# Four double PSUM pairs, keys and queries by pairs of strips, and products with ones over two chunks, in a two-layer attention kernel

## The chip, the cores and the metric

The kernel runs on one core of one Trainium2 chip. The metric is the device time of one execution in microseconds; lower is better. The engines are TensorE (PE, with its weight loads PEld), VectorE (DVE), ScalarE (ACT), GpSimd (POOL) and SyncE (SP), which here issues the DMA transfers.

## The reference

The input is 16 images of 64 x 64 positions with 256 channels, all fp32. Two pre-normalised residual layers follow each other. Cut to what matters:

```python
# layer 0: linear attention, 8 heads of 32
q, k, v = split(norm(x) @ w_qkv)
q = softmax(q, over the 32 channels of a head) * SCALE
k = softmax(k, over the 4096 positions)
context = einsum('bhdn,bhen->bhde', k, v)
x = x + einsum('bhde,bhdn->bhen', context, q) @ w_out
# layer 1: local attention in a window of 7 x 7
q, k, v = xn @ Wq + bq, xn @ Wk + bk, xn @ Wv + bv      # xn = norm(x)
score = q . (k[in window] + row or column embedding)     # emb0, emb1: half the channels each
out = x + sum over the window of softmax(score) * v      # positions outside are zero-padded
```

The norm is a group norm per image. Its mean and deviation are folded by the kernel into the weights and biases of layer 1.

## The kernel before, in words

An image is held as two tiles `img` of 128 channels x 4096 positions and handled in 8 strips of 512 positions. The order of instructions on each engine is the order of the program text; no planner moves them. A loop over the 16 images (L1018 to L1103) runs these stages one after the other:

- **Layer 0** (`layer0`). Queries and keys of two blocks of 128 positions at a time (L531), ScalarE's exponential into a `work` tile `eq` (L535), context sums (L549), the turned queries (L593 to L614), the output products (L642) and DVE's adds into `img` (L653, L656). Statistics of the strips follow, and from them mean and deviation (`group_stats`, which runs `group_steps`: products with a grouping matrix at L268 and L277, small DVE steps at L265, L270, L274, L279).
- **Positional products** (`positional_products`, L695; `positional`). Their bias comes from `fold_bias` (PE L677, DVE's subtract L679), and the values' bias `bv` from a product at L1036 and a DVE subtract (L1039). `store_rings` (L724) writes the result to DRAM.
- **Values** (`values`, L743). For the strips in the order `KEYED` = 2, 3, 4, 5, 6, 7, 1, 0 (called i = 0 to 7) PE makes 16 products into two PSUM banks, DVE adds `bv` (L746) into a `work` tile `v4`, and SP stores that tile to DRAM (L751; the last strip with eight small transfers, L756). After i = 3 SP issues the eight transfers of `load_rings(0)` (L731, L732).
- **Fold** (`fold_bias` twice, L677): the biases of keys (columns 0, 1) and of queries (columns 2, 3), in one PSUM bank.
- **Two halves of local attention**, four heads each (hg = 0, 1). `keys_queries` (L771) makes first all keys, then all queries, two strips at a time; ScalarE (L684) and DVE (L686) evacuate 32 x 512 pieces through `evacuate`, into `kaug` (keys) and `qq` (queries). The last pair of queries is put off until the first scores are issued. `local_attention` then presets masks (L951) and goes through 4 units x 5 groups of two chunks: `scores` (L834) with an exponential on ScalarE into a `work` tile `e` (L843 for hg = 0, L846 for hg = 1), one step later the products with the values (`weighted`, L878; mask L885), DVE's sum of neighbouring chunks (`both_chunks`, L863), and two steps later the products with ones (`summed`, L908). `finish` (L915 to L942) turns the sums and has POOL write the result, which SP stores (L1063). The windows of values are loaded by `load_window` (L804).
- Between groups, `between0` and `between1` (L1065, L1083) load the next image, take its strip statistics (L465), compute its mean and deviation and normalise its first two strips (L285).

PSUM's eight banks are two double tiles `pd` and four single ones `ps`. `psum2()` alternates between the doubles, `bank()` gives the first half of one of them, and `banks()` goes round all four sets. `outs` and `zs` of the attention are the singles. The SBUF pool `work` hands out its buffers in turn; a tile waits until all that used the buffer before is done:

```python
work = ctx.enter_context(tc.tile_pool(name="work", bufs=6))
def work_tile(name):
    return work.tile([P, 1024], F32, tag="work", name=name)
```

The `eq`, `v4` and `e` tiles all come from it.

Of the kernel before, what the change touches and what calls it, by code (L numbers as in the profile page):

```python
# [19 lines left out]
P = 128  # L20
# [22 lines left out]
ORDER = (4, 5, 6, 7, 0, 1, 2, 3)  # L43
EDGE = (5, 3)
# [44 lines left out]
class Net:  # L89
# [28 lines left out]
    def positions(self, psum, work_tile):  # L118
# [8 lines left out]
        both = work_tile("wq_both").rearrange("p (a k c) -> p a k c", a=2, k=2)  # L127
# [129 lines left out]
    def group_steps(self, stats, eps, small, psum, name, result):  # L257
# [5 lines left out]
        mean_c, var_c = mv[:, :, 0:1], mv[:, :, 1:2]  # L263
        rhs = small.tile([P, 2, 1], F32, tag="gn1", name=f"gn1{name}")
        nc.vector.tensor_copy(rhs, mean_c)  # L265
        yield
        pm = psum(f"pm{name}")
        nc.tensor.matmul(pm[:, 0:2], self.grp, rhs.rearrange("p a b -> p (a b)"), start=True, stop=True)  # L268
# [3 lines left out]
        nc.vector.tensor_tensor(d, rhs.rearrange("p a b -> p (a b)"), mean, ALU.subtract)  # L272
        nc.vector.tensor_tensor(d, d, d, ALU.mult)
        nc.vector.tensor_tensor(d, d, var_c.rearrange("p a b -> p (a b)"), ALU.add)  # L274
# [83 lines left out]
def attention_fast(tc, io, ok):  # L358
# [3 lines left out]
    with ExitStack() as ctx:  # L362
# [3 lines left out]
        double = [ps.tile([P, 2, 512], F32, tag=f"pd{i}", name=f"pd{i}") for i in range(2)]  # L366
        single = [ps.tile([P, 512], F32, tag=f"ps{i}", name=f"ps{i}") for i in range(4)]
        turn = [0, 0]

        def psum2():  # L370
            turn[0] += 1
            return double[turn[0] % 2]

        def banks():

            i = turn[1] % 4
            turn[1] += 1
            if i >= 2:
                return single[2 * i - 4 : 2 * i - 2], (0, 1)
            return [double[i][:, j] for j in range(2)], (i, i)  # L380
# [4 lines left out]
        def next_bank(name):  # L385

            return double[(turn[0] + 1) % 2][:, 0, 64:]
# [43 lines left out]
        work = ctx.enter_context(tc.tile_pool(name="work", bufs=6))  # L431
# [4 lines left out]
        def work_tile(name):  # L436
            return work.tile([P, 1024], F32, tag="work", name=name)
# [77 lines left out]
        def layer0(b, x, xn, mean, rstd, xtok, ready, midway=None):  # L515

            mu = None
            pc, other = single[:2], single[2:]
# [7 lines left out]
            def queries_keys(p):  # L526
# [7 lines left out]
                e = work_tile(f"eq{b}_{p}").rearrange("p (t c) -> p t c", t=2)  # L534
# [76 lines left out]
            for hg in range(2):  # L611
                for h in range(4):
                    rows = slice(HD * h, HD * h + HD)
                    nc.tensor.matmul(  # L614
                        double[h // 2][:, h % 2, hg * C : (hg + 1) * C],
                        ch[rows, hg * P : (hg + 1) * P],
                        n.wout_sb[rows, hg],
                        start=True,
                        stop=True,
                    )  # L620
# [3 lines left out]
            for h in range(2):  # L624
                nc.vector.tensor_copy(w4[:, h].rearrange("p g c -> p (g c)"), double[0][:, h])
            nc.scalar.copy(w4[:, 2:4].rearrange("p h g c -> p h (g c)"), double[1])
# [5 lines left out]
            for i in range(NS // 2):  # L632
# [3 lines left out]
                for co in range(2):  # L636
                    py = [double[a // 2][:, a % 2, : 2 * P] if co else single[a][:, : 2 * P] for a in range(4)]
                    for h in range(4):
                        for hg in range(2):
                            for a in range(4):  # L640
                                rows = slice(HD * a, HD * a + HD)
                                nc.tensor.matmul(  # L642
                                    py[a],
# [6 lines left out]
                    if co:  # L650
                        for a in (0, 2):
                            part = double[a // 2][:, :, : 2 * P].rearrange("p a (t n) -> p a t n", n=HD)
                            nc.vector.tensor_tensor(xv[:, a : a + 2], part, xv[:, a : a + 2], ALU.add)  # L653
                    else:
                        for a in range(4):
                            nc.vector.tensor_tensor(xv[:, a], py[a].rearrange("p (t n) -> p t n", n=HD), xv[:, a], ALU.add)  # L656
# [35 lines left out]
        def positional_products(i, x, pair):  # L692
            for k in range(2):
                for a in range(2):
                    nc.tensor.matmul(  # L695
                        single[i][64 * a : 64 * a + 64],
                        wpos[:, k],
                        x[k][:, strip(pair[a])],
                        start=(k == 0),
                        stop=(k == 1),  # L700
                    )

        def positional(i, pair):


            for a in range(2):
                for hg in range(2):
                    rows = slice(64 * a + 32 * hg, 64 * a + 32 * hg + 32)
                    image = placed(qq[32 * hg : 32 * hg + 32, 0], hg)
                    for _, _, m, w, view in pieces(pair[a]):  # L710
                        src = view(single[i][rows])
# [22 lines left out]
        def values(b, s, x):  # L734

            pv, _ = banks()
            v4 = work_tile(f"v4_{b}_{s}").rearrange("p (t c) -> p t c", c=C)
            for i in range(2):
                pi = pv[i].rearrange("p (t c) -> p t c", c=C)
                for t in range(2):  # L740
                    n0 = s * 512 + (2 * i + t) * P
                    for k in range(2):
                        nc.tensor.matmul(pi[:, t], x[k][:, n0 : n0 + P], wv[:, k], start=(k == 0), stop=(k == 1))  # L743
            for i in range(2):
                pi = pv[i].rearrange("p (t c) -> p t c", c=C)
                nc.vector.tensor_tensor(v4[:, 2 * i : 2 * i + 2], pi, bv.unsqueeze(1).to_broadcast([P, 2, C]), ALU.add)  # L746
# [13 lines left out]
        def keys_queries(b, hg, x):  # L760

            for what in range(2):
                for i in range(0, NS, 2):
                    if what and i == NS - 2:
                        yield
                    ps, engines = banks()
                    pair = KEYED[i : i + 2]
                    wgt = wq if what else wk
                    for a in range(2):
                        for k in range(2):  # L770
                            nc.tensor.matmul(  # L771
                                ps[a],
                                wgt[:, k, hg * P : (hg + 1) * P],
                                x[k][:, strip(pair[a])],
                                start=(k == 0),
                                stop=(k == 1),
                            )
                    for a in range(2):
                        for h in range(4):
                            rows = slice(h * HD, (h + 1) * HD)  # L780
                            d0 = 64 * (h % 2)
                            for u, p0, m, w, view in pieces(pair[a]):
                                src = view(ps[a][rows])
                                if what:
                                    dst = placed(qq[d0 : d0 + HD, h // 2], hg)[:, :, w : w + m]
                                else:
                                    dst = kaug[h // 2][d0 : d0 + HD, u, PAD : PAD + W, p0 : p0 + m]
                                dst = by_rows(dst, src)
                                if what and hg:

                                    order = "p r w -> p w r" if len(src.shape) == 3 else "p g r w -> p w g r"
                                    dst, src = dst.rearrange(order), src.rearrange(order)
                                evacuate(engines[a], dst, src, bias[rows, 2 * what + hg : 2 * what + hg + 1])
# [13 lines left out]
        def local_attention(b, hg, x, y, vw, queries, after_scores, between, stored):  # L807
# [3 lines left out]
            outs, zs = single[:2], single[2:]  # L811
# [5 lines left out]
            def scores(t, c):  # L817
# [23 lines left out]
                e = work_tile(f"e{b}_{hg}_{t}_{c}")[:, : 4 * m]  # L841
# [48 lines left out]

            def summed(c, e):
# [18 lines left out]
            def finish(i, t, r, pvs):  # L910

                for k in range(2):


                    nc.vector.transpose(r[:, k], zs[k])  # L915
# [32 lines left out]
            for i in range(4):  # L948
                rows = slice(32 * i, 32 * i + 32)
                to = double[i // 2][:, i % 2]  # L950
# [3 lines left out]
            for step in range(len(groups) + 4):  # L954
                new = None
                if step < len(groups):
                    i, g = groups[step]
                    new = (i, g, [(c, scores(UNITS[i], c)) for c in range(2 * g, min(2 * g + 2, NB))])
# [4 lines left out]
                if held:  # L963
                    i, g, es = held
                    for c, e in es:
                        weighted(c, e, vw[i])
                    if g == 4:
                        rs[i] = [tail.tile([P, 2, 512], F32, tag=f"tail{k}", name=f"r{b}_{hg}_{i}_{k}") for k in range(2)]
                        for j in range(2):
                            nc.scalar.copy(rs[i][1][:, j], outs[j])  # L970
# [3 lines left out]
                if late:  # L974
                    i, g, es = late
                    for c, e in es:
                        summed(c, e)
# [16 lines left out]
        with tc.manual_schedule(engines=ORDERED):  # L994
# [23 lines left out]
            for b in range(B):  # L1018
# [6 lines left out]
                pairs = [ORDER[i : i + 2] for i in range(0, NS, 2)]  # L1025
                positional_products(0, x, pairs[0])
                pb = bank("fold")
                fold_bias(mean, wpos, (4,), pb)
                scale(wv, wv, rstd)
                for i in range(4):  # L1030
                    if i < 3:
                        positional_products(i + 1, x, pairs[i + 1])
                    positional(i, pairs[i])
                pv = bank("foldv")
# [5 lines left out]
                store_rings()  # L1040
                for i, s in enumerate(KEYED):
# [6 lines left out]
                pb = bank("fold2")  # L1048
                fold_bias(mean, wk, (0, 1), pb)
                fold_bias(mean, wq, (2, 3), pb)  # L1050
                vw = {i: load_window(b, 0, UNITS[i]) for i in range(2)}
# [31 lines left out]
                def between1(i, g):  # L1083
# [9 lines left out]
                    if i == 1 and g < 4:  # L1093
                        for s in ORDER[2 * g : 2 * g + 2]:
                            strip_stats(st, x_next, 0, s)
                    if i == 2 and g == 0:
                        steps = n.group_steps(st, 1e-5, small, next_bank, f"0_{b + 1}", gn)
                    if i == 2 and g < 3:
                        next(steps, None)
                    if i == 3 and g in (1, 2):  # L1100
                        normalise(xn_next, x_next, *gn, ORDER[g - 1])
# [389 lines left out]
```

## Time and profile before

| | |
|---|---|
| three runs | 5876.85, 5888.22, 5892.97 us; median 5888.22 us |
| profiled execution | 5892.37 us, span 5890.5 us |
| busy share of PE, PEld, DVE, ACT, POOL | 89%, 61%, 58%, 37%, 23% |
| mean granted clock of TensorE | 0.954 |
| HBM traffic | 371.04 MB read, 158.73 MB written |

Busy shares are averages over stages with different limits. The granted clock is a share of full speed. In a line of a view, an entry such as "L834 PE MATMUL pd<-qq,kaug" is line 834 of the kernel, the engine, the operation, and the tiles written and read, without buffer numbers. "PE pd L951 <- ACT qq L684" means that PE's instruction at L951 waited for ScalarE's at L684.

### The profile page before, as it was taken

What the parts mean: (1) busy time and instruction counts of PE and PEld (TensorE: products, weight loads), DVE (VectorE), ACT (ScalarE), POOL (GpSimd) and SP (SyncE); (2) the same over time, 40 slices, a digit from 0 to 9 for tenths busy, and PEclk for the clock granted to TensorE, in tenths of its full rate; (3) what the DMA queues carried; (4) which work ended last, traced back from release to release, by engine and by line L of the source; (5) the groups of instructions that cost most, each with busy time, mean ns of one, the idle gap of its engine ahead of it and who ended that gap; (6) DMA issues with size and microseconds to landing.
All of it is one profiled execution on the core that took longest, in us unless ns stands there. A gap on an engine that the chain in (4) does not pass through costs nothing.

```text
span 5890.5 us, 169110 instructions
## 1 busy us (share of the span) xinstructions
PE 5235.4 (89%) x75313; PEld 3609.8 (61%) x75313; DVE 3439.0 (58%) x5946; ACT 2193.7 (37%) x3089; POOL 1335.2 (23%) x1946
## 2 busy tenths in 40 slices
PE   7889898898998989989889998988989989899997
PEld 4656566566665666656656666565665666656665
DVE  4565655656565565655655556565574655656555
ACT  1341624425144251442514325144351433514335
POOL 3031231302212022130221302213032130321303
PEclk9999999999999999999999999999999999999999
DMA  4543616445173451734517345173451734517344
GB/s 121 107 102 56 133 54 116 101 74 119 42 130 96 76 115 35 131 94 77 117 33 131 94 77 117 33 133 92 79 119 32 136 86 81 114 35 135 87 77 86
DMA packets 751604, 540.80 MB, mean 92 GB/s; under 512 B 241408, under 2 KB 682368, under 8 KB 748416
## 3 DMA queue, kind: packets, MB, share of 16 engines
q1 hardware_dynamic: 750864, 529.89, 44.1%
q8 instruction: 592, 9.70, 0.7%
q14 instruction: 148, 1.21, 0.1%
HBM read 371.04 MB, written 158.73 MB: 90 GB/s over the span
## 4 chain that ended last, share of the span: by engine, by line
PE 77%; DVE 8%; ACT 5%; issue 5%; DMA 2%; SPq 1%; POOL 1%; DVEq 0%; ACTq 0%; POOLq 0%
PE pd L531 15%; PE pd L834 13%; PE ps L878 8%; PE pd L771 7%; PE ps L549 6%; PE ps L771 5%; ACT qq L684 4%; PE ps L642 4%; PE pd L743 4%; PE pd L642 4%; PE ps L743 4%; PE ps L908 4%; DVE e L863 3%; PE ps L695 2%; DMA vpad<-v 1%
## 5 line engine op out<-in xcount | busy, mean ns | idle before, releaser
L863 DVE TENSOR_TENSOR e<-e,e 128x384 f32<-128x384 f32 x1024 | 732.4, 742 | 773.1 <-PE ps L878 615.2
L834 PE MATMUL pd<-qq,kaug 64*64 64x112 f32 (+4 forms) x27648 | 938.0, 277 | 159.8 <-issue 71.1
L834 PEld LDWEIGHTS pd<-qq,kaug 64*64 64x64 f32 x27648 | 813.2, 139 | 319.5 <-issue 181.8
L531 PE MATMUL pd<-wqkv,img 128*128 128x512 f32 x2048 | 948.8, 608 | 3.2 <-DVE img L285 3.2
L443 POOL TENSOR_TENSOR others<-others,rc 128x32 f32<-128x32 f32 x128 | 32.1, 251 | 2858.6 <-DVE rc L919 2858.4
L535 ACT ACTIVATE eq<-pd 128x1024 f32<-128x1024 f32 x256 | 261.9, 1023 | 1077.7 <-PE pd L531 1077.7
L531 PEld LDWEIGHTS pd<-wqkv,img 128*128 128x128 f32 x2048 | 399.1, 196 | 412.1 <-issue 376.6
L878 PE MATMUL ps<-e,vw 128*32 128x112 f32 (+1 forms) x18432 | 575.2, 261 | 65.2 <-issue 64.5
L538 DVE TENSOR_REDUCE qz<-eq 128x16 f32<-128x512 f32 x256 | 175.5, 686 | 766.9 <-ACT eq L535 766.9
L846 ACT ACTIVATE e<-pd 128x896 f32<-128x896 f32 (+2 forms) x576 | 461.4, 836 | 430.5 <-PE pd L834 423.5
L843 ACT ACTIVATE e<-pd 128x896 f32<-128x896 f32 (+2 forms) x576 | 462.4, 838 | 400.7 <-PE pd L834 395.8
L684 ACT ACTIVATE qq<-ps,bias 32x512 f32<-32x512 f32 (+2 forms) x512 | 318.6, 648 | 733.5 <-PE ps L695 668.6
L908 PE MATMUL ps<-e,ones 128*32 128x128 f32 (+2 forms) x10240 | 404.2, 266 | 146.3 <-DVE e L863 113.0
L878 PEld LDWEIGHTS ps<-e,vw 128*32 128x32 f32 x18432 | 419.0, 114 | 154.4 <-issue 117.5
L942 POOL TENSOR_TENSOR img<-img,r 128x320 f32<-128x320 f32 (+1 forms) x512 | 493.2, 993 | 0.0
L549 PE MATMUL ps<-xtok,eq 128*128 128x257 f32 x2048 | 483.4, 380 | 0.0
L549 PEld LDWEIGHTS ps<-xtok,eq 128*128 128x128 f32 x2048 | 387.4, 190 | 149.8 <-issue 107.1
L684 ACT ACTIVATE kaug<-pd,bias 32x512 f32<-32x512 f32 x256 | 173.7, 678 | 674.8 <-PE pd L771 671.9
L686 DVE TENSOR_SCALAR qq<-ps,bias 32x512 f32<-32x512 f32 (+2 forms) x416 | 312.3, 759 | 151.0 <-PE ps L771 145.2
L934 POOL TENSOR_TENSOR r<-r,r 128x512 f32<-128x512 f32 x256 | 340.7, 1352 | 140.5 <-DVE r L921 134.8
L908 PEld LDWEIGHTS ps<-e,ones 128*32 128x32 f32 x10240 | 253.3, 116 | 189.6 <-DVE e L863 148.1
L465 DVE BATCH_NORM_STATS2 st<-img 128x6 f32<-128x512 f32 x512 | 332.1, 679 | 9.7 <-DMA img<-in_xc 5.2
(128 smaller groups left out, 6609.9 us busy)
## 6 DMA issues: line engine op xcount, KB each, us to landing
vw<-vpad SPq DMA_DIRECT2D x512, 288.0 KB
img<-in_xc SPq DMA_DIRECT2D x256, 256.0 KB
xtok<-in_xt SPq DMA_DIRECT2D x64, 1024.0 KB
out<-img SPq DMA_DIRECT2D x256, 256.0 KB
vpad<-v SPq DMA_DIRECT2D x112, 512.0 KB
qq<-pos SPq DMA_DIRECT2D x128, 256.0 KB
qq<-in_ring SPq DMA_DIRECT2D x128, 256.0 KB
pos<-qq SPq DMA_DIRECT2D x128, 112.0 KB
```

The source lines that it names most:

```text
L531: nc.tensor.matmul(ps[:, t], xn[k][:, n0 : n0 + P], n.wqkv_sb[:, k, : 2 * C], start=(k == 0), stop=(k == 1))
L549: nc.tensor.matmul(pc[hg][:, : C + 1], eq[p][:, t, C + hg * P : C + (hg + 1) * P], xtok[p // 4][:, 2 * (p % 4) + t], start=(p == 0 and t = ...
L642: nc.tensor.matmul(py[a], w4[rows, h, hg, co * P : (co + 1) * P], qv[rows, 4 * hg + h, 8 * HD * i : 8 * HD * (i + 1)], start=(h == 0 and h ...
L684: nc.scalar.activation(dst, src, AF.Identity, bias=bias)
L743: nc.tensor.matmul(pi[:, t], x[k][:, n0 : n0 + P], wv[:, k], start=(k == 0), stop=(k == 1))
L771: nc.tensor.matmul(ps[a], wgt[:, k, hg * P : (hg + 1) * P], x[k][:, strip(pair[a])], start=(k == 0), stop=(k == 1),)
L834: nc.tensor.matmul(to, kaug[pl][rows, u, 8 * c : 8 * c + 8].rearrange("p r w -> p (r w)"), q, start=True, stop=True,)
L843: nc.scalar.activation(e.rearrange("p (a n) -> p a n", a=2), ps[:, :, : 2 * m], AF.Exp)
L863: nc.vector.tensor_tensor(part, part, rows_of(c - 1, before, r0, 8 * c), ALU.add)
L878: nc.tensor.matmul(dst, stationary, pr, **flags)
L908: nc.tensor.matmul(dst, ones, pr, start=True, stop=True)
L942: nc.gpsimd.tensor_tensor(yv, xv, by_rows(add[:, :, a - w0 : e - w0], xv), ALU.add)
```

## The change

- The PSUM banks become four double tiles `pairs`. `psum2()` alternates between the first two; layer 0's sums, `outs` and `zs` use the last two. The positional products lie in the first bank of each pair, their bias in the second bank of `pairs[2]`, the values' bias in the second bank of `pairs[1]`, the biases of keys and queries in the first bank of `pairs[1]`.
- `work` has three buffers of 1792 columns where it had six of 1024. The two chunks of a group share one `e` tile.
- `values` makes one DVE add of 1024 columns per strip. The first two windows of values are loaded after i = 5 and i = 6.
- `keys_queries` takes the strips in the pairs (0, 1), (2, 3), (4, 5), (6, 7), keys and queries in turn; a piece of 32 rows covers both strips of a pair, except those of the pair with strip 0. Keys go to DVE, queries to ScalarE; the last pair of queries, which is put off, to both.
- Products with ones: for g = 1 and 3, four matmuls over both chunks (`summed_both`).
- Layer 0's output adds are two of 512 columns for both channel halves (before, the first half had four of 256). The copy of the means in `group_steps` is gone. `finish` turns 1024 columns at once, and a unit's result is copied by ScalarE at once.
- `between1` takes one strip's statistics per step, and one half strip's normalisation per step.

The diff, cut to its core:

```diff
-        double = [ps.tile([P, 2, 512], F32, tag=f"pd{i}", name=f"pd{i}") for i in range(2)]
-        single = [ps.tile([P, 512], F32, tag=f"ps{i}", name=f"ps{i}") for i in range(4)]
+        pairs = [ps.tile([P, 2, 512], F32, tag=f"pair{i}", name=f"pair{i}") for i in range(4)]
...
-        work = ctx.enter_context(tc.tile_pool(name="work", bufs=6))
+        work = ctx.enter_context(tc.tile_pool(name="work", bufs=3))
...
-            return work.tile([P, 1024], F32, tag="work", name=name)
+            return work.tile([P, 2 * PART], F32, tag="work", name=name)
...
-            pv, _ = banks()
-            v4 = work_tile(f"v4_{b}_{s}").rearrange("p (t c) -> p t c", c=C)
...
+            pv = pairs[KEYED.index(s) % 4].rearrange("p i (t c) -> p (i t) c", c=C)
+            v4 = work_tile(f"v4_{b}_{s}")[:, :1024].rearrange("p (t c) -> p t c", c=C)
+            for t in range(4):
+                n0 = s * 512 + t * P
+                for k in range(2):
+                    nc.tensor.matmul(pv[:, t], x[k][:, n0 : n0 + P], wv[:, k], start=(k == 0), stop=(k == 1))
+            nc.vector.tensor_tensor(v4, pv, bv.unsqueeze(1).to_broadcast([P, 4, C]), ALU.add)
...
-            for what in range(2):
-                for i in range(0, NS, 2):
...
+            for i in range(8):
+                pair, what = QUERIED[i // 2], i % 2
+                wgt = wq if what else wk
+                ps = pairs[i % 4]
+                if i == 7:
+                    yield
...
+                    engine = h // 2 if i == 7 else i % 2
...
+            def summed_both(c, both, a, z):
+
+                i, n = a // 32, 14
+                for h in range(4):
...
+                    nc.tensor.matmul(dst, ones, pr, start=True, stop=True)
...
-                pb = bank("fold")
+                pb = pairs[2][:, 1]
...
-                pv = bank("foldv")
+                pv = pairs[1][:, 1]
...
+                    if i in (5, 6):
+                        vw[i - 5] = load_window(b, 0, UNITS[i - 5])
-                pb = bank("fold2")
+                pb = pairs[1][:, 0]
                 fold_bias(mean, wk, (0, 1), pb)
                 fold_bias(mean, wq, (2, 3), pb)
-                vw = {i: load_window(b, 0, UNITS[i]) for i in range(2)}
...
-                    if i == 1 and g < 4:
-                        for s in ORDER[2 * g : 2 * g + 2]:
-                            strip_stats(st, x_next, 0, s)
-                    if i == 2 and g == 0:
+                    at = 5 * i + g - 3
+                    if 0 <= at < NS:
+                        strip_stats(st, x_next, 0, ORDER[at])
+                    if at == NS:
                         steps = n.group_steps(st, 1e-5, small, next_bank, f"0_{b + 1}", gn)
-                    if i == 2 and g < 3:
+                    if NS <= at < NS + 3:
                         next(steps, None)
-                    if i == 3 and g in (1, 2):
-                        normalise(xn_next, x_next, *gn, ORDER[g - 1])
+                    if i == 3 and g < 4:
+                        k, o = g % 2, strip(ORDER[g // 2])
+                        n.normalise(xn_next[k][:, o], x_next[k][:, o], *gn, k)
```

## The prediction

> **What bounds the kernel now.** I read the page's shares first, then the chain and the clock, then PE's waits, then one image stage by stage. From the page, busy time by engine and the chain that ended last; from the view of cores, the clock:
>
> ```profile
> PE 5235.4 (89%) x75313; PEld 3609.8 (61%) x75313; DVE 3439.0 (58%) x5946; ACT 2193.7 (37%) x3089; POOL 1335.2 (23%) x1946
> PE 77%; DVE 8%; ACT 5%; issue 5%; DMA 2%; SPq 1%; POOL 1%; DVEq 0%; ACTq 0%; POOLq 0%
> core 0: 5890.5 us, clock 0.954
> ```
>
> PE is busy 89% of the span and carries 77% of the chain: it sets the time. An edit counts only where it fills or opens a gap on PE, shortens PE's work, or changes its clock. The 16 images take about 365 us each; PE's gaps are about 38 us of that. PE's waits (line, what ended the wait: total us, times, longest):
>
> ```profile
> PE pd L268 <- DVE gn L265: 77.8, 21, 19.9
> PE pd L951 <- ACT qq L684: 55.5, 27, 2.4
> PE pd L834 <- ACT e L843: 30.6, 16, 1.9
> PE pd L834 <- ACT e L846: 28.8, 16, 1.8
> PE pd L834 <- DVE gnm L270: 21.0, 15, 2.1
> PE pd L743 <- DVE bvn L1039: 17.2, 8, 2.5
> PE pd L951 <- DMA vw<-vpad: 11.8, 5, 2.4
> ```
>
> L951 and L834 are the start of each attention (32 of them): evacuations still on ACT hold up the masks and then the first exponentials. L743 is the start of `values` in every second image. Now three stages of the image that starts its values at 3464.9: values, `keys_queries` of half 0, and the first score groups:
>
> ```profile
> 3464.50:3494.50 30.00, 29.48 (x164) 25.68 (x162) 14.21 (x25) 3.82 (x4) 0.00 (x0) 1.00 0.91 151
> 3494.50:3521.90 27.40, 25.05 (x60) 10.66 (x60) 20.92 (x28) 18.05 (x29) 0.00 (x0) 0.98 1.08 189
> 3521.90:3535.60 13.70, 11.79 (x174) 7.80 (x176) 3.55 (x5) 9.09 (x17) 0.00 (x0) 0.75 0.39 106
> ```
>
> The columns are length, busy PE, PEld, DVE, ACT, POOL, granted clock, DMA share, GB/s. The first two are PE-bound at full clock, with the DMA engines full (0.91, 1.08); the third runs at 0.75 of the clock. PE's timeline where values hand over to keys:
>
> ```profile
> 3492.58 0.65 PE L677 MATMUL pd<-gnm,w 128*64 128x1 f32 x16
> 3493.50 0.65 PE L677 MATMUL pd<-gnm,wqn 128*64 128x1 f32 x16 [0.26 <-DVE bias L679]
> 3494.41 5.85 PE L771 MATMUL pd<-img,w 128*128 128x512 f32 x13 [0.25 <-DVE bias L679]
> ```
>
> The second bias fold waits 0.26 for DVE's subtract (L679) of the first, as both use one bank. Whatever holds DVE up at that point holds PE. From SP's timeline there, three issues:
>
> ```profile
> 3480.20 1.16 SPq L731 DMA_DIRECT2D qq<-pos  x1
> ...
> 3495.91 1.29 SPq L751 DMA_DIRECT2D vpad<-v  x2
> ...
> 3506.65 0.53 SPq L756 DMA_DIRECT2D vpad<-v  x1
> ```
>
> The four stores of strips i = 0 to 3 are issued before 3480.2, then the eight ring loads, and the store of strip i = 4 (the fifth) only at 3495.9. SP's issues go round eight completion semaphores; the sixth store of the last strip, at 3506.65, needs the one of strip 4's store. So that store landed at 3506.6, 41.8 us after the start of values. The semaphore increments in the record give the same for every image: 39.7 to 43.1, mean 40.8; store 0 lands at 12 to 15. Last, VectorE's durations (mean ns after the busy us):
>
> ```profile
> L656 DVE TENSOR_TENSOR img<-ps,img 128x256 f32<-128x256 f32 x256 | 90.7, 416 | 99.5 <-PE ps L642 99.5
> L746 DVE TENSOR_TENSOR v<-pd,bvn 128x512 f32<-128x512 f32 x128 | 82.4, 686 | 155.1 <-PE pd L743 155.1
> L679 DVE TENSOR_TENSOR bias<-biases,pd 128x2 f32<-128x2 f32 x32 | 4.8, 151 | 12.0 <-PE pd L677 12.0
> ```
>
> From 416 and 686 at 256 and 512 columns, 1024 take an estimated 0.69 + 0.54 = 1.23 us.
>
> **What the Trainium skill says.** "TensorE: Matmul & The Clock Gate", Part 1: an idle window of about 3.4 us (free-running) halves PE's clock, and about 3.4 us of work restores it. The trace agrees, and is stricter: after gaps of 1.8 us or more the clock is 0.5 for stretches of about 3.4 us, so such a gap costs some 1.7 us besides itself. "DMA: Bandwidth & Descriptors", Queues, rings and completion order: SP's transfers share one ring on each DMA engine and are consumed in ring order. The trace agrees: store 4, issued at 31.0, lands at 41.8, behind the ring loads, where store 0, issued at 11.3, took 3.3 us.
>
> **The change, part by part (us per image).**
>
> *The values tiles.* `work` falls from six buffers to three, so the tile of strip i takes the one of strip i - 3. The last strip's add (i = 7) then cannot start before the store of strip 4 has landed; with six it waited for store 1, which landed at about 16. Behind that add in DVE's order stand the bias subtracts, then all key evacuations; behind the first subtract stands PE's second bias fold, and behind that all of `keys_queries`. Timetable from the start of values: first fold ends at 28.5; store 4 lands at about 41.5 (the mean of the images without the L743 wait is 41.2; strip 3's own add now waits for store 0 and passes on up to 1 us to the ring loads); add 1.23, subtract 0.15, hand-overs 0.15: PE resumes at 43.0 to 43.3. Wait **14.5**, bounds 13.5 (landing as in the mean of all) to 16.5 (as in the latest). After it the clock is at half once: +1.7, bounds 0 and 3.4. After that PE needs 3.4 us a pair and DVE about 5 us per two pairs, so PE does not wait again. Sum **+16.2**. Loading the windows early buys nothing here: they stand in SP's queue behind store 4 and were not late.
>
> *Bias of values.* The fold and the positional products lie in other banks, so L743's wait goes: 17.2 / 16 = **-1.1**. Every image then looks like the odd ones, which start values at once. Late next would be SP's stores, which nothing on PE waits for.
>
> *Starts of attention.* 72 evacuations per half become 48 and the last deferred pair has four wide ones, shared by ACT and DVE. ACT takes 0.68 for 32x512 and about 1.15 for 1024 (estimate from 1.02 for 128x1024 and 0.68). In the steady rhythm ACT's last queries end about 0.9 after PE wants the bank, then the first exponentials 0.7: 1.6 per attention, where the waits above give (55.5 + 11.8 + 30.6 + 28.8) / 32 = 3.96. Gain 2.4 twice = 4.7; with most of these gaps under 1.8, about half of the half-clock time after them goes, 1.6. **-6.3**, bounds -8 (all half clock gone) and -3 (the wide pieces are no quicker for ACT).
>
> *Between the groups of half 1.* Strip statistics one per step instead of two, group steps a step later, normalise one half per step. In these steps PE has waits of 0.9 (L268), 1.6 (L834 <- DVE gnm), a drain of up to 2.7 (L908 <- DVE e) and up to 10 us at half clock. I take **-3.5**, bounds 0 (the same DVE work merely lies elsewhere) and -5.5.
>
> *Exponentials in pairs, three tiles.* An exp of group n now waits for DVE's last read of group n - 2's first half. In the trace that slack is 0.8 in most groups and negative by up to 0.9 in some five per attention: **+1.0**, bounds 0 and 2.
>
> *Ones over two chunks.* For g = 1 and 3, eight matmuls of 128 columns become four of 256. A set of four takes 109 ns a pass at 128 columns and 96 at 112: it goes by columns, so only instruction supply gains, **-0.3** (0 to -1).
>
> *The rest.* The copy of the means leaves the path: -0.2. In one half of layer 0's outputs two adds of 512 (1.37 us) take the place of four of 256 (1.66): nothing, since PE's products for a half, about 3.4 us, cover both; without that cover -0.3, or +0.3 if a pair's banks come free later. Three buffers for layer 0's exponentials leave 2.4 us of slack; the wide transpose and ScalarE copy of a finished unit lie beside scores.
>
> Sum: 16.2 - 1.1 - 6.3 - 3.5 + 1.0 - 0.3 - 0.2 = **+5.8 us per image, +93**. Against the profiled execution's own 5892.4 (span 5890.5) that is 5985; the median of runs, 5888.2, lies 4.2 below, so **5981**. Taking the bounds together (not all at the same end) gives +1 to +10.5 per image: 5905 to 6056.
>
> **Rivals.**
> 1. *The store is not waited for* (it lands before DVE reaches the last add, or something reorders it): everything but the first term stands, 5.8 - 16.2 = -10.4, -166: **5722**, faster. It decides once store 4 lands by 27.5. For it: nothing but that the DMA queue could drain sooner; against it: 16 of 16 images at 39.7 or later, with DMA engines full.
> 2. *The wait is there, but the gains are larger*: starts -8, between -5.5, waits on tiles 0, no half clock after the long gap: 14.5 - 1.1 - 8 - 5.5 - 0.5 = -0.6, about -10: **5878**, within or just past no change. The break-even is 16 us of gains; the gaps of PE, 38 us, would allow it.
> 3. *The gains fail*: ACT and DVE are as late as before and the steps of half 1 only shift: starts -3, between 0, the rest as in the sum: 16.2 - 1.1 - 3 + 1 - 0.5 = +12.6, +202: **6090**. For it: DVE, busy 20.9 of 27.4 us in `keys_queries`, gets no less to do per column.
>
> **How the numbers follow.** A measurement of this kernel can tell about 0.3%, 18 us, from no change (its three runs lie 16 apart). Chances: my forecast 0.66, rival 1 0.10, rival 2 0.12, rival 3 0.12. The range 5880 to 6075 holds nearly all of the forecast, the upper part of rival 2 and the lower half of rival 3, and leaves rival 1 out. Faster takes rival 1 and half of rival 2, 0.16; same 0.07; slower the rest, 0.77.
>
> **What would show it.** In the changed profile: one PE wait of 14 to 15 us per image at the fold before keys, put down to DVE's bias, some 230 in total; DVE's values add waiting for a DMA of the stores; L743's wait gone; 20 to 60 in place of 127 for the waits at the start of attention; PE busy about as many us. If the fold does not wait, the forecast is wrong at its first term; if it does and the time still falls, the other terms are too small.

## The result, and the profile after

The changed kernel takes 6134.6 us (median of 4 runs, 6117.69 to 6142.63), the kernel before 5890.6 beside it: ratio 1.0422, interval 1.0393 to 1.0451. It is slower, as forecast, but by 244 us where the forecast said 93 and the range ended at 6075. The profiled execution's span is 6115.9 us, 225 above the one before.

The page of the changed kernel, shares of busy time, and the view of cores:

```profile
PE 5263.1 (86%) x73265; PEld 3572.0 (58%) x73265; DVE 3416.3 (56%) x5338; ACT 1999.0 (33%) x2385; POOL 1353.1 (22%) x1946
core 0: 6115.9 us, clock 0.933
```

PE's busy time rose by 28 us although it has 2048 matmuls fewer, and the clock fell from 0.954 to 0.933. Of the 225 us of longer span, then, 28 are longer busy time at a lower clock, and some 198 are time in which PE stands idle. PE's waits (line, what ended them: total us, times, longest):

```profile
PE pair L664 <- DVE bias L666: 216.3, 16, 14.2
PE pair L902 <- DVE e L859: 71.6, 46, 3.0
PE pair L830 <- ACT e L839: 58.9, 16, 4.0
PE pair L830 <- ACT e L842: 55.2, 16, 3.8
PE pair L921 <- DVE e L859: 42.0, 71, 1.1
PE pair L963 <- ACT qq L671: 33.3, 32, 1.3
PE pair L830 <- DVE gnm L270: 19.5, 15, 1.5
PE pair L1051 <- ACT qq L671: 7.4, 16, 0.5
```

The first line is the forecast wait at the second fold: 13.5 us, once in each of 16 images. L963 (masks) fell to 33.3 from 55.5 + 11.8, as forecast, and the wait of `values` for `bv` is gone; at the product for `bv` (L1051) a small one of 0.5 took its place. But the waits of the scores (L830) for the exponentials rose from 30.6 + 28.8 to 58.9 + 55.2, where the forecast had them fall. With the masks, the waits at the starts of attention come to 147 us, where the forecast had 20 to 60 in place of 127. That is what was not seen.

The 16 images, cut into stages at PE's first instruction of each stage in the trace. Each cell has the mean us per image and, after the slash, how much of it lay at half clock, time in which PE waits included. "First three groups" runs from the first scores of a half to the scores of its fourth group. The last three columns are kernels of the experiments below:

| stage | before | after | own buffer | tail on DVE | both |
|---|---|---|---|---|---|
| layer 0 to its output products | 91.2 / 3.8 | 92.0 / 5.7 | 92.0 / 5.5 | 92.0 / 5.3 | 92.2 / 6.0 |
| output products, positional | 47.6 / 8.6 | 47.4 / 10.2 | 47.5 / 10.0 | 47.3 / 9.9 | 47.8 / 10.5 |
| values | 28.0 / 0.2 | 27.8 / 0 | 27.8 / 0 | 27.8 / 0 | 27.8 / 0 |
| fold and keys, queries, half 0 | 28.9 / 0.1 | 43.9 / 17.1 | 28.6 / 0.9 | 44.0 / 17.1 | 28.4 / 0.4 |
| first three groups, half 0 | 13.7 / 3.1 | 15.7 / 4.5 | 16.0 / 5.9 | 11.3 / 0 | 11.3 / 0 |
| other groups, half 0 | 55.2 / 4.5 | 54.0 / 2.6 | 53.9 / 2.6 | 53.7 / 2.2 | 53.7 / 2.0 |
| keys, queries, half 1 | 27.4 / 1.3 | 26.4 / 1.4 | 26.6 / 1.8 | 26.8 / 2.1 | 26.6 / 1.9 |
| first three groups, half 1 | 13.3 / 2.5 | 15.3 / 3.7 | 15.7 / 5.1 | 11.3 / 0 | 11.3 / 0 |
| other groups, half 1 | 61.3 / 9.8 | 58.2 / 6.3 | 59.0 / 7.9 | 60.0 / 6.9 | 60.1 / 9.2 |

Two things carry the result: the fold with the keys and queries of half 0, +15.0, and the two starts of attention (the rows of the first three groups), +2.0 each. For the starts, the masks' waits ahead of them included, the forecast had -6.3.

**The long wait.** PE's timeline in the third image, from values to keys (start, length, engine, line, operation, tiles, in brackets the idle time before it and what ended it):

```profile
964.18 0.65 PE L664 MATMUL pair<-gnm,w 128*64 128x1 f32 x16
978.27 1.04 PE L664 MATMUL pair<-gnm,wqn 128*64 128x1 f32 x16 [13.44 <-DVE bias L666]
979.24 4.63 PE L753 MATMUL pair<-img,w 128*128 128x512 f32 x5
```

DVE's timeline at the same place:

```profile
976.93 1.23 DVE L729 TENSOR_TENSOR v<-pair,bvn 128x1024 f32<-128x1024 f32 x1 [14.87 <-DMA vpad<-v]
978.07 0.15 DVE L666 TENSOR_TENSOR bias<-biases,pair 128x2 f32<-128x2 f32 x1
```

And SP's, ahead of it:

```profile
960.53 4.53 SPq L719 DMA_DIRECT2D qq<-in_ring  x1
965.16 1.28 SPq L734 DMA_DIRECT2D vpad<-v  x2
```

The last add of values waits 14.87 us for a store (`vpad<-v`) to land; SP issued that store, of strip 4, at 965.16, after the last ring load. (Strips are counted here by i, as in the description of the kernel.) The subtract follows, then PE. Each link stands as the forecast had it, and the add takes 1.23 us as estimated. By the semaphore that the add waits on, strip 4's store landed 40.1 to 41.1 us after the start of values in the 16 images, 40.4 on average.

**The start of attention.** ScalarE's timeline around the put-off pair of queries in half 1 of the third image:

```profile
1105.43 1.55 ACT L842 ACTIVATE e<-pair 128x512 f32<-128x512 f32 x2 [1.15 <-PE pair L830]
1112.41 2.22 ACT L671 ACTIVATE qq<-pair,bias 32x1024 f32<-32x1024 f32 x2 [5.44 <-DVE qq L673]
1114.66 1.73 ACT L842 ACTIVATE e<-pair 128x896 f32<-128x896 f32 x2
```

DVE's timeline there:

```profile
1109.75 2.56 DVE L673 TENSOR_SCALAR qq<-pair,bias 32x1024 f32<-32x1024 f32 x2 [1.33 <-PE pair L753]
```

And PE's:

```profile
1105.94 3.70 PE L753 MATMUL pair<-img,wqn 128*128 128x512 f32 x8
1109.57 1.56 PE L830 MATMUL pair<-qq,kaug 64*64 64x112 f32 x48
...
1115.63 2.04 PE L830 MATMUL pair<-qq,kaug 64*64 64x112 f32 x48 [3.43 <-ACT e L842]
```

The products of the pair end at about 1109.6, and DVE starts its two pieces. ScalarE does not start its own beside them: it waits for DVE's (`<-DVE qq L673`) until 1112.4, ends at 1114.6, and only then comes the exponential that frees a PSUM pair for the next scores. PE waits 3.43 us, and the granted clock is 0.68 on average over the 3.5 us after that.

### The profile page after: what moved, and what is told of

Same layout as the page of the kernel before. It is cut to its first block, busy times and chain, and to the rows that moved or that the text cites. A ratio compares the mean times of both kernels' runs of the same rounds, so it can differ in the third digit from the quotient of the medians.

```text
span 6115.9 us, 163438 instructions
## 1 busy us (share of the span) xinstructions
PE 5263.1 (86%) x73265; PEld 3572.0 (58%) x73265; DVE 3416.3 (56%) x5338; ACT 1999.0 (33%) x2385; POOL 1353.1 (22%) x1946
## 5 line engine op out<-in xcount | busy, mean ns | idle before, releaser
L671 ACT ACTIVATE qq<-pair,bias 32x1024 f32<-32x1024 f32 (+3 forms) x832 | 678.8, 846 | 1875.4 <-PE pair L682 675.4
L830 PE MATMUL pair<-qq,kaug 64*64 64x112 f32 (+4 forms) x27648 | 936.8, 278 | 198.6 <-issue 61.0
L830 PEld LDWEIGHTS pair<-qq,kaug 64*64 64x64 f32 x27648 | 817.5, 139 | 398.6 <-issue 185.0
L522 PE MATMUL pair<-wqkv,img 128*128 128x512 f32 x2048 | 949.2, 609 | 5.7 <-DVE img L285 5.7
L673 DVE TENSOR_SCALAR kaug<-pair,bias 32x1024 f32<-32x1024 f32 (+3 forms) x768 | 689.0, 922 | 248.3 <-PE pair L753 242.7
L874 PE MATMUL pair<-e,vw 128*32 128x112 f32 (+1 forms) x18432 | 565.1, 259 | 55.0 <-issue 55.0
L842 ACT ACTIVATE e<-pair 128x896 f32<-128x896 f32 (+2 forms) x576 | 463.2, 835 | 427.5 <-PE pair L830 364.8
L839 ACT ACTIVATE e<-pair 128x896 f32<-128x896 f32 (+2 forms) x576 | 463.1, 836 | 421.2 <-PE pair L830 334.8
L753 PE MATMUL pair<-img,w 128*128 128x512 f32 x1024 | 515.3, 651 | 0.0
L540 PE MATMUL pair<-xtok,eq 128*128 128x257 f32 x2048 | 483.4, 380 | 0.0
L633 PE MATMUL pair<-qq,w 32*128 32x256 f32 x8192 | 469.5, 388 | 12.5 <-DVE w L616 12.5
L633 PEld LDWEIGHTS pair<-qq,w 32*128 32x128 f32 x8192 | 423.8, 193 | 60.7 <-DVE w L616 21.8
```

The costliest lines, as they stand in the source:

```text
L522: nc.tensor.matmul(ps[:, t], xn[k][:, n0 : n0 + P], n.wqkv_sb[:, k, : 2 * C], start=(k == 0), stop=(k == 1))
L540: nc.tensor.matmul(pc[hg][:, : C + 1], eq[p][:, t, C + hg * P : C + (hg + 1) * P], xtok[p // 4][:, 2 * (p % 4) + t], start=(p == 0 and t = ...
L633: nc.tensor.matmul(py[a // 2][:, a % 2], w4[rows, h, hg, co * P : (co + 1) * P], qv[rows, 4 * hg + h, 8 * HD * i : 8 * HD * (i + 1)], star ...
L671: nc.scalar.activation(dst, src, AF.Identity, bias=bias)
L673: nc.vector.tensor_scalar(dst, src, bias, None, ALU.add)
L753: nc.tensor.matmul(ps[:, a], wgt[:, k, hg * P : (hg + 1) * P], x[k][:, strip(pair[a])], start=(k == 0), stop=(k == 1),)
```

## The experiments

Theory A: the long wait comes, all of it, from the tile of the last strip's values, which waits for a store. Theory B: two engines that evacuate one PSUM tile take turns, and that delays the exponentials. In the diffs, long lines are wrapped, and "..." marks what is left out.

**An own buffer for the last strip's values (changed kernel).**

```diff
-            v4 = work_tile(f"v4_{b}_{s}")[:, :1024].rearrange("p (t c) -> p t c", c=C)
+            v4 = work_tile(f"v4_{b}_{s}")[:, :1024] if s else tail.tile(
+                [P, 2, 512], F32, tag="tail0", name=f"v4_{b}_{s}").rearrange("p a b -> p (a b)")
+            v4 = v4.rearrange("p (t c) -> p t c", c=C)
```

> The changed kernel, with the values tile of the last strip (i = 7) in a buffer of its own (one that is idle in that stage), so that its add waits for no store. Theory A: the 13.5 us wait of PE at the second fold, once per image, comes only from that add waiting for the store of strip 4; it goes, with the half-clock time behind it: keys_queries of half 0 falls from 43.9 to about 29 us, the time by 15 x 16 = 240 us, ratio to before 1.00. Rival: the wait moves on (to the key evacuations, or to the ring loads' arrival): under half of it comes back, ratio 1.02 to 1.04.

Measured: 5898.3 us, ratio 1.0040 (1.0026 to 1.0054). The fold's wait has shrunk from 216.3 to 12.8 us in total, 0.8 each:

```profile
PE pair L664 <- DVE bias L666: 12.8, 16, 0.8
```

The fold with the keys and queries of half 0 takes 28.6 us. DVE's adds of values now wait mostly for PE's products (first line); their waits for stores (second line) are 31.8 us in total, against 262.1 in the changed kernel:

```profile
DVE v L730 <- PE pair L729: 232.8, 116, 2.4
DVE v L730 <- DMA vpad<-v: 31.8, 12, 3.0
```

Theory A holds: 0.038 of the 0.042 comes from this one tile. The waits for stores that remain are short, and none of them is at the last strip.

**The same wait alone, in the kernel before.** The first attempt let each values tile skip a place of the rotation:

```diff
+            work_tile(f"v4_{b}_{s}_skipped")
             v4 = work_tile(f"v4_{b}_{s}").rearrange("p (t c) -> p t c", c=C)
```

> The kernel before, with every values tile taking two places of the rotation of six, so that strip i waits for the store of strip i - 3; nothing else differs. Theory A: the whole cost of the wait comes back by itself, +13.5 to 15 us per image: 5890 + 216 to 240, ratio 1.037 to 1.041. Rival: the wait needs the new bank plan (one fold bank, one pair per strip): ratio under 1.01.

Measured: 5882.0, ratio 1.0006 (0.9989 to 1.0022). The result tells nothing for either theory, since the edit did not make the wait: by the semaphores in the trace, the adds of the last two strips wait for the stores of strips 0 and 1, six strips back, as in the kernel before. A tile that is never used held no place back. The second attempt names the buffers:

```diff
-            v4 = work_tile(f"v4_{b}_{s}").rearrange("p (t c) -> p t c", c=C)
+            k = KEYED.index(s) % 3
+            v4 = (tail.tile([P, 2, 512], F32, tag=f"tail{k}", name=f"v4_{b}_{s}").rearrange("p a b -> p (a b)")
+                  if k < 2 else work_tile(f"v4_{b}_{s}"))
+            v4 = v4.rearrange("p (t c) -> p t c", c=C)
```

> The kernel before, with the values tiles in two idle buffers and one of the rotation, in turn, so that the last strip's tile waits for the store of strip 4; nothing else differs. Theory A: the cost of the wait by itself, 13.5 to 15 us per image, ratio 1.037 to 1.041. Rival: the wait needs the new bank plan as well (here keys of strips 2 and 3 have other banks than the last strip's): a third of it or less, ratio up to 1.013.

Measured: 6140.7, ratio 1.0436 (1.0394 to 1.0478). PE's first wait in this kernel's list:

```profile
PE pd L677 <- DVE bias L679: 216.6, 16, 15.1
```

And DVE's for stores:

```profile
DVE v L748 <- DMA vpad<-v: 281.5, 27, 17.1
```

The same 16 waits with the same total (216.6 and 216.3), without any other part of the change. The new bank plan is not needed for it, nor are the windows of values that the change loads earlier.

**The put-off pair by strips (changed kernel).** Strip 6 to DVE, strip 7 to ScalarE (numbered by position here), four pieces each; both strips still lie in one PSUM tile, in a bank each.

```diff
-                    if pair[0]:
+                    if pair[0] and i < 7:
...
-                            evacuate(engine, dst, src, b0)
+                            evacuate(a if i == 7 else engine, dst, src, b0)
```

> The changed kernel, with the put-off pair of queries evacuated by strip (strip 6 by VectorE, strip 7 by ScalarE, four 32x512 pieces each) instead of by rows (two 32x1024 pieces each). Theory B: ScalarE's two pieces wait for VectorE's two because both read the same two PSUM banks, so the third group's exponentials come 2.6 us late; with a bank each, ScalarE ends its four pieces about 2.9 us after the pair, not 4.9: PE's wait for the exponential falls from 3.5 to about 1.5 per attention, 32 x 2 = 64 us and some half-clock time, ratio 1.025 to 1.032. Rival: the wait is one of writes into the same tile of queries, and stays: ratio 1.042.

Measured: 6171.9, ratio 1.0517 (1.0500 to 1.0535), slower still. ScalarE's timeline at the same place:

```profile
1113.82 0.68 ACT L671 ACTIVATE qq<-pair,bias 32x512 f32<-32x512 f32 x1 [3.55 <-DVE qq L673]
1115.31 0.68 ACT L671 ACTIVATE qq<-pair,bias 32x512 f32<-32x512 f32 x1 [0.81 <-DVE qq L673]
```

DVE's beside it:

```profile
1113.05 0.74 DVE L673 TENSOR_SCALAR qq<-pair,bias 32x512 f32<-32x512 f32 x1 [1.33 <-PE pair L753]
1114.53 0.74 DVE L673 TENSOR_SCALAR qq<-pair,bias 32x512 f32<-32x512 f32 x1 [0.75 <-ACT qq L671]
```

Now the engines take turns piece by piece, through all eight pieces, and PE's waits for the exponentials grow to 75.6 + 71.7 us. The wait doesn't go by banks: theory B in that form fell. Left were the PSUM tile, and the tile of queries that both engines write.

**The put-off pair in two PSUM tiles (with the own buffer).** Strip 7's products go to the third pair, and ScalarE evacuates them; the queries are written as in the kernel by strips.

```diff
+                each = [ps[:, 0], pairs[2][:, 0] if i == 7 else ps[:, 1]]
...
-                            ps[:, a],
+                            each[a],
...
-                            evacuate(engine, dst, src, b0)
+                            evacuate(a if i == 7 else engine, dst, src, b0)
```

> The changed kernel with the values tile repaired; of the put-off pair, strip 6 is computed in the fourth PSUM pair and evacuated by VectorE, strip 7 in the third pair and evacuated by ScalarE, into the same tile of queries as ever. Theory B, now: the engines take turns because both read one PSUM tile, whatever the rows or banks. Then ScalarE starts when the products end, PE's wait for the exponential falls from 3.5 to 1 to 2 per attention, ratio 0.987 to 0.995 where the repaired kernel has 1.004. Rival: the turns come from writing one tile of queries; then ScalarE still waits for VectorE and the ratio is 1.004 or more.

Measured: 5822.2, ratio 0.9895 (0.986 to 0.993). ScalarE's timeline of this kernel:

```profile
1055.78 2.75 ACT L671 ACTIVATE qq<-pair,bias 32x512 f32<-32x512 f32 x4 [3.52 <-PE pair L755]
```

DVE's:

```profile
1053.74 3.03 DVE L673 TENSOR_SCALAR qq<-pair,bias 32x512 f32<-32x512 f32 x4
```

They work side by side from 1055.78 to 1056.77, and ScalarE's wait ends with PE's products, no longer with DVE's last piece. Only the PSUM tile differs from the kernel by strips here, apart from the own buffer, so the wait goes by the PSUM tile. It is a wait in the program: in the changed kernel and in the one by strips, ScalarE's piece waits on a semaphore that DVE's piece raises. PE's waits for the exponentials are down to two of 1.3 us. The starts take 12.2 and 12.4 us, about one more than in the two kernels below that use DVE alone, because the masks at L883 now wait for ScalarE's pieces to leave the third pair:

```profile
PE pair L883 <- ACT qq L671: 47.2, 32, 1.6
```

**The put-off pair on DVE alone (changed kernel).**

```diff
-                    engine = h // 2 if i == 7 else i % 2
+                    engine = 0 if i == 7 else i % 2
```

> The changed kernel, with the put-off pair of queries evacuated by VectorE alone (four 32x1024 pieces, 5.1 us). Theory B: no exponential stands behind an evacuation any more, PE's wait of 3.5 us for it at the start of each attention goes, with half-clock time: 32 x 3.5 to 5 = 110 to 160 us, ratio 1.015 to 1.023. Rival: VectorE's sums of chunks now come 2.5 us later and PE waits for them at the products with ones instead: ratio 1.035 to 1.042.

Measured: 6004.4, ratio 1.0216 (1.0187 to 1.0245). PE's waits for exponentials have left the list, and both starts take 11.3 us, none of it at half clock. The rival's wait is there, but small: L921 for DVE's sums rose from 42.0 to 55.6 us, and L921 waits another 11.7 us for DVE's pieces of the queries.

**Both repairs: the own buffer, and the put-off pair on DVE alone (changed kernel).**

> The changed kernel with both repairs: the last strip's values tile in a buffer of its own, and the put-off pair of queries evacuated by VectorE alone. If the two costs are independent, 240 us and 130 us come off 6134: 5765, ratio to before 0.98. Rival: with the long wait gone the starts of attention are bound by something else (masks, windows), and the two repairs share a gain: ratio 0.99 to 1.00.

Measured: 5770.6, ratio 0.9805 (0.9771 to 0.984): the two costs add up (1.0422 - 0.0382 - 0.0206 = 0.9834, inside the interval), and this kernel is faster than the one before as well. Its page:

```profile
PE 5200.8 (90%) x73265; PEld 3510.3 (61%) x73265; DVE 3501.3 (61%) x5402; ACT 1922.5 (33%) x2321; POOL 1353.6 (23%) x1946
```

**The put-off pair on DVE alone, in the kernel before.**

```diff
-                                evacuate(engines[a], dst, src, bias[rows, 2 * what + hg : 2 * what + hg + 1])
+                                evacuate(0 if what and i == NS - 2 else engines[a], dst, src,
+                                         bias[rows, 2 * what + hg : 2 * what + hg + 1])
```

> The kernel before, with the put-off pair of queries (strips 1 and 0, twelve pieces) evacuated by VectorE alone; nothing else differs. Theory: most of what the repaired kernel gains at the starts of attention comes from having no evacuation on ScalarE ahead of the second group's exponentials, not from the wide pieces: PE's wait of 1.8 to 1.9 there goes with its half-clock time, 2 per attention, 32 x 2 = 64 us, ratio 0.987 to 0.992. Rival: VectorE's twelve pieces take 7.5 us and delay the sums of chunks, for which PE then waits: ratio 0.997 or more.

Measured: 5819.8, ratio 0.9892 (0.9863 to 0.9921). The starts take 11.9 and 11.3 us instead of 13.7 and 13.3, and PE's waits for the exponentials there fall from 59.4 us to 1.0. So over half of the gain of the repaired kernel (0.0108 of 0.0195) is to be had in the old plan, by one argument.

**The steps between groups put back (with both repairs).** The edit takes back the diff of `between1` (the last part of the diff of the change).

> The kernel with both repairs, and the steps of the next image between the groups of half 1 put back as before (two strips of statistics in a step, group steps one step earlier, two normalisations in a step). From the stage after the third group of half 1, 61.3 us before and 58.2 with the change: the old order costs 3 us per image, 48 us, ratio 0.8% above the kernel with both repairs. Rival: those 3 us came from other edits (products with ones, tiles in pairs): no difference, within 0.3%.

Measured: 5781.2, ratio 0.9823 (0.979 to 0.9856), against 0.9805 with the new order: not told apart. Its other groups of half 1 take 60.7 instead of 60.1.

**Ones chunk by chunk again (with both repairs).**

```diff
-                    if g in (1, 3):
+                    if g in ():
```

> The kernel with both repairs (ratio 0.98), with the products with ones of every group chunk by chunk again, eight matmuls of 128 columns for g = 1 and 3 where it has four of 256. The prediction's term: PE time goes by columns, so 0.3 us per image (0 to 1), ratio 0.981. Rival: the 1.5 us that the stage after the third group of half 0 lost with the change, and part of half 1's, come from these products (fewer instructions to supply, fewer waits for sums of chunks): 1.5 to 3 us per image, ratio 0.985 to 0.989.

Measured: 5794.2, ratio 0.9841 (0.9818 to 0.9863). That is 0.0036 above the repaired kernel, some 21 us or 1.3 per image. The intervals overlap (0.9818 to 0.9863, and 0.9771 to 0.984), so a gain from the wide products is likely, but neither its size nor the prediction's 0.3 per image is settled. The other groups of half 0 take 55.7 instead of 53.7, at half clock for 4.2 instead of 2.0. PE's waits for the sums of chunks are of about the same total (125.3 against 77.4 + 55.1), so they don't explain it; whether the supply of instructions or the clock does was not told apart.

## Why the prediction was wrong

- **Values tiles: right.** The wait was put at 14.5 (13.5 to 16.5), and at 16.2 with the clock. It is 13.5, at the lower bound, and the stage grew by 15.0. The timetable had the store of strip 4 land at 41.5; it landed at 40.4, and that is the difference.
- **Starts of attention: the step that failed.** It was -6.3, with bounds of -8 and -3. Measured is +2.0 + 2.0 for the starts and -1.0 for the keys and queries of half 1, where the masks' waits lie: +3.0. (The masks' waits of half 0 lie in the row with the fold.) The 9.3 between them make some 149 us. The profiled execution is longer by 225 us where the forecast said 93, so it missed by 132: this term alone is more than the whole miss, and the other terms together took a little of it back. The masks' part was right. The sentence that failed is that the last pair's pieces are "shared by ACT and DVE": it took them to run side by side, with ScalarE done 0.9 us after PE wants the bank and 0.7 more for the exponential. They run one after the other, 2.6 and then 2.2 us, so PE waits 3.4 to 4.0 us at each of the 32 starts. The bounds were built from the widths of the pieces and left no room for an order between the engines; the program's waits had that order in them. The Trainium skill, "PSUM — Partial Sum Buffer", section "PSUM bank collisions raise a hardware error", says that the compiler's scheduler adds a dependency between two engines that touch the same bank and the same quadrant of 32 partitions, reads included. Here the engines read different quadrants (DVE the first 64 partitions, ScalarE the others) and in the kernel by strips different banks. This program orders them all the same, so the rule by which it was built is the coarser one. With one engine for all of the pair the term comes near the forecast: -2.4 - 2.0 - 0.8 = -5.2 with both repairs. That is not the forecast's mechanism come true, since ScalarE then has no piece at all; and the old plan with the pair on DVE alone has -1.8 - 2.0 for the starts without wide pieces.
- **Bias of values: half right.** 1.1 of wait went; 0.5 came back at L1051, and the two stages gained 0.4 together. The step missed that the product for `bv` now shares a PSUM tile with a positional bank that ScalarE is still reading.
- **Between the groups, -3.5: not shown.** The stage fell by 3.1 in the changed kernel. But with both repairs it fell by 1.2 only, and there taking the new order back costs about 0.7, which the intervals don't tell from nothing. Of the waits that the term named, the one for `gnm` hardly moved (21.0 to 19.5 us in all). What else made the stage shorter stays open.
- **Ones, -0.3: perhaps too small.** The experiment has 1.3, with intervals that overlap. If it is 1.3, going by columns can't be the reason, since the columns are the same.
- **Tiles in pairs, +1.0: half seen.** The exponentials do wait for DVE's reads of an `e` tile now, 66.7 us in all where it was 2.2 before. But PE's waits for the sums of chunks are 113.0 before and 71.6 + 42.0 after, and its waits for exponentials all lie at the starts, so no cost on PE shows. It was not tried alone.
- **Layer 0, at nothing:** +0.9, with 2 us more at half clock. The waits for one of the turned copies (`ct`) rose from 9.7 to 15.9 us in all. One tile where two singles were is a likely cause, but that is only argued.
- **The clock after a gap: read too broadly.** The prediction took every gap of 1.8 us or more to be followed by about 3.4 us at half clock. In the trace of the kernel before, 88 of PE's 144 gaps of that length have a stretch at half clock that starts in the gap or within 3.5 us after it, and the stretches last 3.4 us (59 of 104) or 6.8 us (38).

The rival with failing gains, 6090, came nearest, but by luck: it has ScalarE as late as before, where in fact it is later. The rival without the store's wait, 5722, can be held against the kernel with the own buffer, in which that wait is removed: 5898, mainly because the starts were not what it assumed.

## What to carry to other kernels

When a pool gets fewer buffers, list for each tile whose end it now waits for; if that is a DMA, look up where in its queue it stands, and what is queued behind the waiting instruction. When banks are merged into larger tiles, list every place where two engines read one tile: in this program they take turns there, even on different partitions and banks. On a kernel bound by TensorE, keep the engine that frees its next bank clear of everything else.

## What the runs showed of the hardware

PE's gap of about 3.5 us at the start of attention costs more than itself. In the changed kernel, each of the 32 gaps (3.4 to 4.0 us) is followed by a stretch at half clock, of 3.4 us in 23 cases and of 6.8 in 9. With the pair on DVE alone, each start fell by 4.0 to 4.4 us, and its time at half clock (3.7 to 4.5 us) went to nothing. The waits of 1.5 us on average (1.6 at most) that the kernel with two PSUM tiles has in the same place brought no half clock there. One wide DVE pass of 32x1024 takes 1.28 us where two of 32x512 take 1.49 (0.747 each), and ScalarE 1.17 where two of queries took 1.42 (0.71 each), so at these shapes the wide pieces save 14 to 18% of the evacuation time.
